# Reordering the rounds of the context-and-routing stage of a fused attention and mixture-of-experts kernel

## The chip, the core and the metric

The kernel runs on one core of a Trainium2 chip. The metric is the device time of one launch in microseconds (us). A core has five engines, each with an instruction queue of its own that it works through in order: TensorE (PE in the profile, its weight loads PEld), VectorE (DVE), ScalarE (ACT), GpSimd (POOL) and SyncE (SP, which here only issues transfers). Engines wait for one another through semaphores.

## What is computed

Tokens x are 32 sequences of 56 rows of 256 numbers; each sequence has a context of 1500 x 256. Four steps follow one another, each added to x:

1. A decayed scan over the context, projected in and out and averaged over time. Since everything in it is linear, it is one weighted sum of the 1500 context rows per sequence, times one 256 x 256 matrix, plus a constant row. The normalized x plus this row is normalized again.
2. A mixture of 16 experts (hidden width 176); every token goes to its best 6 of 16 by a softmax gate.
3. Attention of the tokens over their own context, with a mask.
4. A mixture of two experts (hidden width 1024), one per token.

```
x = x + layernorm(layernorm(x) + mean_t(scan(ctx W_in + b_in) W_out + b_out))
x = x + sum over the best 6 of 16 of score_e * expert_e(layernorm(x))
x = x + softmax(layernorm(x) ctx^T / 16, masked) ctx
x = x + score_best * expert_best(layernorm(x))
```

## The kernel before, in words

The change lies in the first stage, which does step 1 and sorts the tokens for step 2. Its loop runs over 16 pairs of sequences (`for p in range(NP)`, lines 653 to 697); a pair is a tile of 128 rows, 56 tokens in each half. The steps of one pair are spread over several rounds of the loop, and each round calls steps of pairs p, p-1, p-2 and p-3:

- `count_in(b)`, L350: PE sums the 1500 rows of context b with the scan's weights into `acc` in PSUM, 12 matmuls. Contexts lie in a ring of five buffers in SBUF; after context b has been summed, SP issues the load of context b+5 (1536 KB in the profile, L165).
- `sum_out` (ScalarE copies `acc` out, L478), `sum_in_columns` (PE `sp` L484, then `sv`), `projected` (PE `sT` L497, ScalarE `sm` L501), `to_rows` (PE `bp` L505, the row spread to 128 rows).
- `first_stats` and `first_rows`: the first normalization of x, on DVE with two ScalarE roots (Ln, then Exp), and on GpSimd `z` L470 and `xr` L474.
- `first_norm` (DVE `z` L509, statistics L189 and L190, two roots on ScalarE), `residual` (DVE L516, L517, statistics), `second_root` (ScalarE), `second_norm` (GpSimd `xn` L529), `away` (SP stores `xn` to DRAM, L535).
- `turned` (PE transposes `xn`, `tp` L201, ScalarE copies `xT` L203), `gate` (PE `lp` L543), `best` (ScalarE copies the logits L552; DVE takes the six best; ScalarE takes `pr`, an Exp that needs DVE's maximum, L563).
- `ranks` (PE `rk` L568), `counted` (DVE), `places` (DVE, with one scaling on ScalarE): each chosen token's place in its expert's list, as a level and an offset in a block of 128.
- `ones_at(p, h)`: one-hot rows of the offsets, half h of the experts; half 0 and half of half 1 on DVE (L609), the other four experts on GpSimd (L614). `sorted_in` (PE, `owned` L631): one-hots times values, summed over all pairs into the table of blocks.

After the loop come the last pair's steps and the tables of the sorted blocks (lines 698 to 780); then the expert stage gathers rows of `xn` from DRAM (`xb` L956) and multiplies them by the up weights (`gu` L798) and the down weights (`y` L825). The up weights are loaded by four transfers (`load_w0_up`, L214), the down weights by 26 small ones (`w0_down_pieces`, L233).

Within one engine the order of the instructions is what sets the order of the work. PE, DVE, ScalarE and SP run in the order in which the code is written (`manual_schedule`, L90); for GpSimd a scheduler chose the order in the first stage. It put `z` and `xr` of a later pair ahead of `xn` in each round.

Of the kernel before, what the change touches and what calls it, by code (L numbers as in the profile page):

```python
# [19 lines left out]
P = 128  # L20
# [32 lines left out]
LATE = T - WIN  # L53
SPAN = 2048
FAR = 1 << 17
ISC = 1.0 / 16.0


@with_exitstack
def xattn_ffn_kernel(  # L60
# [178 lines left out]
    with tc.tile_pool(name="p1", bufs=1) as p1, tc.tile_pool(name="p3", bufs=3) as p3, tc.tile_pool(  # L239
# [160 lines left out]
                start=(e == 0), stop=False,  # L400
            )
        PE.matmul(vp[:, 0:D], lhsT=ones[0:1, :], rhs=bout_sb, start=False, stop=True)
        cvec = p1.tile([1, D], F32, name="cvec")
        A.copy(cvec, vp[0:1, 0:D])

        sm = p1.tile([3, D], F32, name="sm")
        nc.gpsimd.dma_start(out=sm[2:3], in_=cvec)
        t3 = p1.tile([P, 3], F32, name="t3")
        V.tensor_scalar(t3[:, 0:1], lower, -1.0, 1.0, ALU.mult, ALU.add)
        V.tensor_copy(t3[:, 1:2], lower)  # L410
# [48 lines left out]
        rsa = p1.tile([P, NP], F32, name="rsa")  # L459

        def first_stats(o):
            for p in range(o, o + 4):
                V.bn_stats(out=st[:, p, :], in_=xr[:, p, :])
                V.bn_aggr(out=mva[:, p, :], in_=st[:, p, :])
            inverse_root(rsa[:, o : o + 4], mva[:, o : o + 4, 1])

        def first_rows(o):
            for p in range(o, o + 2):
                zc[p] = zp.tile([P, D], F32, tag="z", name="z")
                G.tensor_scalar(  # L470
                    zc[p], xr[:, p, :], mva[:, p, 0:1], rsa[:, p : p + 1],
                    ALU.subtract, ALU.mult,
                )
                G.tensor_tensor(xr[:, p, :], xr[:, p, :], bet, ALU.add)  # L474

        def sum_out(p):
            acc = p3.tile([P, D], F32, tag="acc", name="acc")
            A.copy(acc, pend[p]["acc"][:, 0:D])  # L478
            keep(p, acc=acc)

        def sum_in_columns(p):
            sp = ps.tile([P, 512], F32, tag="ps", name="sp")
            for k in range(KD):
                PE.matmul(  # L484
                    sp[:, 2 * k : 2 * k + 2], lhsT=pend[p]["acc"][:, k * P : (k + 1) * P],
                    rhs=sel2[:, 0:2], start=True, stop=True,
                )
            sv = p3.tile([P, KD, 2], F32, tag="sv", name="sv")
            V.tensor_scalar(
                sv.rearrange("p k h -> p (k h)"), sp[:, 0 : 2 * KD], 1.0 / T, None, ALU.mult  # L490
            )
            keep(p, sv=sv)

# [14 lines left out]
        def first_norm(p):  # L508
            V.tensor_tensor(zc[p], zc[p], pend[p]["bp"][:, 0:D], ALU.add)  # L509
            mv = stats(zc[p])  # L510
            inverse_root(mv[:, 2:3], mv[:, 1:2])
            keep(p, mv=mv)

        def residual(p):
            mv = pend[p]["mv"]
            V.scalar_tensor_tensor(zc[p], zc[p], mv[:, 0:1], gam, ALU.subtract, ALU.mult)  # L516
            V.scalar_tensor_tensor(  # L517
                xr[:, p, :], zc[p], mv[:, 2:3], xr[:, p, :], ALU.mult, ALU.add
            )
            keep(p, mv=stats(xr[:, p, :]))  # L520
# [45 lines left out]
        def ranks(p):  # L566
            rk = ps.tile([P, 512], F32, tag="ps", name="rk")
            PE.matmul(rk[:, 0:E0], lhsT=before, rhs=sel[:, p, :], start=True, stop=True)  # L568
            PE.matmul(rk[:, E0 : 2 * E0], lhsT=ones, rhs=sel[:, p, :], start=True, stop=True)
            keep(p, rk=rk)  # L570

        def counted(p):

            rk = pend[p]["rk"]
            V.tensor_tensor(pos[:, p, :], rk[:, 0:E0], base0, ALU.add)
            V.tensor_tensor(base0, base0, rk[:, E0 : 2 * E0], ALU.add)

        def places(p):

            nm, pr = pend[p]["nm"], pend[p]["pr"]  # L580
            qi = small.tile([P, E0], I32, tag="qi", name="qi")
            V.tensor_copy(qi, pos[:, p, :])
            V.tensor_scalar(qi, qi, 7, None, ALU.logical_shift_right)
            V.tensor_copy(lvl[:, p, :], qi)

            off = small.tile([P, E0], F32, tag="off", name="off")
            V.scalar_tensor_tensor(
                off, lvl[:, p, :], -float(P), pos[:, p, :], ALU.mult, ALU.add
            )
            V.scalar_tensor_tensor(off, off, 1.0, sel[:, p, :], ALU.add, ALU.mult)  # L590
            v = vals[:, p % 2]
            V.tensor_tensor(
                v[:, :, 0, :], e16.unsqueeze(1).to_broadcast([P, E0, NLP]),
                lvl[:, p, :].unsqueeze(2).to_broadcast([P, E0, NLP]), ALU.is_equal,
            )
            V.reciprocal(nm[:, 1:2], nm[:, 1:2])
            V.scalar_tensor_tensor(
                v[:, :, 1, :], v[:, :, 0, :], nm[:, 1:2],
                pr.unsqueeze(2).to_broadcast([P, E0, NLP]), ALU.mult, ALU.mult,
            )  # L600
            A.activation(v[:, :, 0, :], v[:, :, 0, :], AF.Copy, scale=ids[:, p : p + 1])
            keep(p, off=off)

        def ones_at(p, h):

            off = pend[p]["off"][:, NE * h : NE * h + NE]
            oh = ohp.tile([P, NE, P], F32, tag="oh", name="oh")
            n = NE // 2 if h and p < NP - 1 else NE
            V.tensor_tensor(  # L609
                oh[:, 0:n], iota.unsqueeze(1).to_broadcast([P, n, P]),  # L610
                off[:, 0:n].unsqueeze(2).to_broadcast([P, n, P]), ALU.is_equal,
            )
            for i in range(n, NE):
                G.tensor_scalar(oh[:, i, :], iota, off[:, i : i + 1], None, ALU.is_equal)  # L614
            pend[p].setdefault("hots", []).append(oh)

        def busy(n):

# [19 lines left out]
        lgs = [p1.tile([P, E0 + 2], F32, name=f"lg{i}") for i in range(2)]  # L638
        for lg in lgs:
            G.memset(lg[:, E0 : E0 + 2], -BIG)  # L640
        sum_out(0)
        first_stats(0)
        first_rows(0)
        pieces = list(w0_down_pieces())


# [3 lines left out]
                    pieces.pop(0)()  # L650


        for p in range(NP):
            if p >= 1:
                first_norm(p - 1)
            if p >= 3:
                ones_at(p - 3, 0)
            if p >= 1:
                residual(p - 1)
            if p >= 2:  # L660
                count_in(2 * p)
                count_in(2 * p + 1)
            if p >= 1:
                sum_out(p)
                second_root(p - 1)
            if p >= 2:
                ranks(p - 2)
            sum_in_columns(p)
            if p >= 3:
                ones_at(p - 3, 1)  # L670
            if p >= 1:
                second_norm(p - 1)
                away(p - 1)
                some_pieces(1)
            projected(p)
            if p >= 3:
                sorted_in(p - 3)
            if p >= 1:
                turned(p - 1)
            if p >= 2:  # L680
                counted(p - 2)
                places(p - 2)
            if p >= 1:
                gate(p - 1)
            to_rows(p)
            if p < 3:
                first_stats(4 * p + 4)
            if p == 2:
                table_constants()
            if p >= 1:  # L690
                best(p - 1)
            if p % 2 == 0 and p + 2 < NP:
                first_rows(p + 2)
            if p == NP - 3:
                load_w0_up()
            if p > NP - 3:
                some_pieces(6)
        last = NP - 1
        first_norm(last)
        ones_at(NP - 3, 0)  # L700
        residual(last)
        ones_at(NP - 3, 1)
        second_root(last)
        ranks(NP - 2)
        second_norm(last)
        away(last)
        some_pieces(len(pieces))
        sorted_in(NP - 3, 0)
        turned(last)
        sorted_in(NP - 3, 1)  # L710
        gate(last)
        busy(1)
        counted(NP - 2)
        places(NP - 2)
        best(last)
        ranks(last)
        for h in range(2):
            ones_at(NP - 2, h)
        for h in range(2):
            sorted_in(NP - 2, h)  # L720
        counted(last)


# [7 lines left out]
        at_ = vals[:, NP % 2]  # L731
# [209 lines left out]
    with tc.manual_schedule(  # L941
# [30 lines left out]
        def ways(a, b):  # L972
# [6 lines left out]
            for l in range(levels_of(b - 1)):  # L979
# [8 lines left out]
                ra[:, q], ra[:, q], float(P), pos[:, q], ALU.mult, ALU.add  # L988
            )
            yield lambda: V.scalar_tensor_tensor(  # L990
                ra[:, q], ra[:, q], 1.0 - P, sel[:, q], ALU.add, ALU.mult
            )
            for p in range(a, b):
                yield lambda p=p: V.max(out=t8s[:, p, :], in_=ra[:, p, :])
# [702 lines left out]
```

## Time and profile before

| what | value |
|---|---|
| median of 3 runs | 728.69 us (727.43 to 730.54) |
| the profiled execution: its time | 726.86 us |
| its span, first to last instruction | 725.2 us |
| busy in the span: PE, PEld, DVE, ACT, POOL | 662.7, 441.0, 402.1, 241.8, 348.7 us |
| mean granted PE clock, of full speed | 0.954 |
| count of pair 2 ends, count of pair 15 ends | 52.3 and 175.4 us |
| first gate and up matmul of the expert stage | 209.05 us |
| between these two counts: DMA share, GB/s, PE clock | 0.95, 345, 0.93 |

The profile's page cuts the span into 40 slices of 18.1 us; the first ten are the loop. "DMA" is the mean busy share of the 16 DMA engines, "PEclk" the granted clock of PE, both in tenths in the page. The chain of waits follows the work that ended last back through the engines; the waits list who waited for whom ("43.1, 11, 6.0" is 43.1 us in total, 11 times, 6.0 us the longest).

### The profile page before, as it was taken

To read this page: it belongs to the slowest core of one execution; us is meant where nothing else is said; L and a number is where in the kernel's file an instruction comes from. 1 tells how busy PE (TensorE), PEld (TensorE's weight loads), DVE (VectorE), ACT (ScalarE), POOL (GpSimd) and SP (SyncE) were. 2 spreads that over 40 slices of the span, in tenths; PEclk is the share of its full clock that TensorE was granted. 3 is DMA by queue.
4 is the path that set the end of the run, shared out by engine and by line. 5 is a ranking of instruction groups with operands and counts; after the bars stand their busy time and mean duration, and the time that the engine had idled before them with its cause. 6 is when DMAs were issued, how large, how long until landed. Compare 5 with 4: busy or idle time off the path is not lost.

```text
span 725.2 us, 13538 instructions
## 1 busy us (share of the span) xinstructions
PE 662.7 (91%) x4113; PEld 441.0 (61%) x4113; DVE 402.1 (55%) x1378; ACT 241.8 (33%) x704; POOL 348.7 (48%) x440
## 2 busy tenths in 40 slices
PE   7867888888779999999999999999988999999996
PEld 4534555555447777667777776666644656656664
DVE  7548877788815645535444447677876332322322
ACT  0123333333124444444444443566551111111110
POOL 7164665554154457567766776568342202212111
PEclk8869998999579999999999999999999999999999
DMA  8998999899527999545554554796931201111000
GB/s 313 309 358 344 369 358 339 320 387 306 152 66 232 266 331 294 172 137 158 152 154 131 163 156 132 204 290 128 351 127 52 58 8 44 29 31 43 22 30 18
DMA packets 70657, 136.62 MB, mean 188 GB/s; under 512 B 7732, under 2 KB 43205, under 8 KB 70581
## 3 DMA queue, kind: packets, MB, share of 16 engines
q1 hardware_dynamic: 56036, 100.31, 40.2%
q0 software_dynamic: 14544, 35.37, 18.3%
q8 instruction: 38, 0.62, 0.4%
q14 instruction: 39, 0.31, 0.1%
HBM read 109.54 MB, written 26.77 MB: 188 GB/s over the span
## 4 chain that ended last, share of the span: by engine, by line
PE 79%; DVE 11%; POOL 3%; ACT 3%; issue 2%; DMA 2%; POOLq 0%; DVEq 0%
PE gu L798 29%; PE y L825 18%; PE acc L360 7%; PE tp L816 5%; PE tp L201 4%; PE tp L926 2%; PE sp L1155 2%; PE owned L631 2%; PE op L1190 1%; PE bp L505 1%; PE lp L543 1%; DVE st L189 1%; POOL xn L529 1%; DVE oh L609 1%; DMA sm<-cvec 1%
## 5 line engine op out<-in xcount | busy, mean ns | idle before, releaser
L798 PE MATMUL gu<-w_sb,xT 128*128 x380 | 131.1, 467 | 3.5 <-issue 1.3
L804 ACT ACTIVATE sg<-gu 128x176 f32<-128x176 f32 (+1 forms) x155 | 53.2, 343 | 229.8 <-PE gu L798 225.9
L956 POOL DMA_INDIRECT xb<-xn,idx x95 | 91.4, 962 | 62.4 <-PE tp L201 39.3
L798 PE MATMUL gu<-ring,xT 128*128 x240 | 112.9, 593 | 0.6 <-issue 0.6
L810 DVE SCALAR_TENSOR_TENSOR hs<-sg,wgt,gu 128x176 f32<-128x176 f32 x95 | 37.7, 397 | 120.3 <-ACT sg L804 120.3
L825 PE MATMUL y<-w_sb,hT 88*128 x380 | 97.9, 379 | 0.0
L798 PEld LDWEIGHTS gu<-w_sb,xT 128*128 128x128 f32 x380 | 71.5, 192 | 30.6 <-ACT xT L203 2.9
L869 POOL DMA_INDIRECT g<-ys,early x78 | 74.6, 956 | 30.0 <-issue 14.7
L808 DVE TENSOR_TENSOR hs<-sg,gu 128x256 f32<-128x256 f32 x60 | 25.2, 420 | 112.2 <-ACT sg L804 112.2
L1441 POOL DMA_INDIRECT out<-ob,ti x15 | 14.8, 989 | 127.2 <-DVE ob L1438 126.9
L816 PEld LDWEIGHTS tp<-ident,hs 128*88 128x88 f32 (+1 forms) x310 | 39.9, 130 | 58.7 <-issue 46.7
L825 PEld LDWEIGHTS y<-w_sb,hT 88*128 88x128 f32 x380 | 64.5, 190 | 5.7 <-issue 0.6
L798 PEld LDWEIGHTS gu<-ring,xT 128*128 128x128 f32 x240 | 45.3, 190 | 33.1 <-issue 30.2
L818 DVE COPY hT<-tp 88x256 f32<-88x256 f32 (+1 forms) x155 | 64.3, 415 | 0.2 <-PE tp L816 0.2
L825 PE MATMUL y<-ring,hT 128*128 x240 | 61.7, 380 | 0.0
L203 ACT COPY xT<-tp 128x256 f32<-128x256 f32 x126 | 47.0, 373 | 44.0 <-PE tp L201 43.0
L816 PE MATMUL tp<-ident,hs 128*88 128x128 f32 (+1 forms) x310 | 59.3, 273 | 0.2 <-DVE mv L884 0.2
L360 PE MATMUL acc<-ring,cz 128*32 128x256 f32 x768 | 53.5, 434 | 0.2 <-DVE cz L321 0.2
L964 ACT COPY yb<-y 128x256 f32<-128x256 f32 x95 | 35.4, 372 | 42.8 <-PE y L825 41.4
L201 PE MATMUL tp<-ident,xb 128*128 128x128 f32 x220 | 42.3, 274 | 2.3 <-issue 2.3
L825 PEld LDWEIGHTS y<-ring,hT 128*128 128x128 f32 x240 | 41.0, 190 | 3.3
L360 PEld LDWEIGHTS acc<-ring,cz 128*32 128x32 f32 x768 | 27.4, 124 | 24.0 <-issue 11.6
(309 smaller groups left out, 1007.1 us busy)
## 6 DMA issues: line engine op xcount, KB each, us to landing
ring<-in_cx SPq DMA_DIRECT2D x32, 1536.0 KB
ys<-yb SPq DMA_DIRECT2D x95, 128.0 KB
ring<-in_cx SPq DMA_DIRECT2D x16, 384.0 KB
extra<-in_cx SPq DMA_DIRECT2D x16, 384.0 KB
xs<-zrow SPq DMA_DIRECT2D x5, 771.0 KB
w_sb<-in_wg SPq DMA_DIRECT2D x2, 1408.0 KB
w_sb<-in_wu SPq DMA_DIRECT2D x2, 1408.0 KB
xn<-xn SPq DMA_DIRECT2D x16, 128.0 KB
```

The costliest lines, as they stand in the source:

```text
L201: PE.transpose(tp[:, k * P : (k + 1) * P], xn[:, k * P : (k + 1) * P], ident)
L203: A.copy(xT.rearrange("p k c -> p (k c)"), tp[:, 0 : KD * P])
L360: PE.matmul(acc[Q * g : Q * g + Q, 0:D], lhsT=cz[:, j, 1 - h : 1 - h + Q], rhs=c[:, j, :], start=(h == 0 and m == 0), stop=(h == 1 and m = ...
L798: PE.matmul(gu[:, 0 : 2 * fp], lhsT=xT[i][:, k, :], rhs=w[:, bass.ds(at[i] + (u * piece + k * 2 * fp), 2 * fp)], start=(k == 0), stop=(k = ...
L804: A.activation(sg, gu[:, 0:fp], AF.Silu)
L810: V.scalar_tensor_tensor(hs[i, u], sg, wgt[:, i : i + 1], up, ALU.mult, ALU.mult)
L816: PE.transpose(tp[0:h, c * P : (c + 1) * P], a[:, c * h : (c + 1) * h], ident)
L818: V.tensor_copy(hT[i, u], tp[0:h, 0 : 2 * P])
L825: PE.matmul(y[i][:, 0:D], lhsT=a[:, c * P : (c + 1) * P], rhs=w[0:h, bass.ds(at[i] + (u * piece + doff + c * D), D)], start=(u == 0 and c ...
L869: G.indirect_dma_start(out=g, out_offset=None, in_=ys0[0 : n * P, :], in_offset=bass.IndirectOffsetOnAxis(ap=at[:, p, k : k + 1], axis=0),)
L956: G.indirect_dma_start(out=xb, out_offset=None, in_=xn0, in_offset=bass.IndirectOffsetOnAxis(ap=idx[:, i : i + 1], axis=0),)
L964: A.copy(yb, y[:, 0:D])
```

## The change

Each round's calls are put in another order, and parts of the steps are changed:

- GpSimd's order in the loop is fixed, as written: `xn`, one-hots, then `z` and `xr` of pair p+2.
- The contexts of pair p+1 are summed in round p, in two pieces: the first between `projected` and `to_rows`, the second after `residual`. Before, both contexts of pair p were summed in one piece in round p.
- `to_rows` and `first_norm` of pair p come in the middle of round p, `residual(p)` behind them; before, `first_norm` and `residual` of pair p-1 stood at the start of round p.
- `sum_out(p)` is the first call of a round. The call before it is the end of the round before: `best`, then `first_stats` (now two pairs in each of rounds 0 to 6, not four pairs before the loop and in rounds 0 to 2).
- `sorted_in` is called by halves.
- All pieces of the down weights come in rounds 13 to 15 and behind them; before, one came in each of rounds 1 to 15, six more in each of rounds 14 and 15, and what was left after that. The up weights are issued in round 12, not 13.
- The bias row goes straight into `sm` by one ScalarE copy of three rows, without a transfer.
- Level and offset of a place are worked out by adding and subtracting a large constant in float; the casts to integer and the shift go. Positions are multiplied by `sel` at once and count from one.
- `sv` is made on ScalarE, not on DVE.
- After the loop the steps of pairs 13 to 15 are reordered too; one of the four spare matmul groups (`busy`) goes, and a scratch tile lies in the context ring.

The core of the diff:

```
-        cvec = p1.tile([1, D], F32, name="cvec")
-        A.copy(cvec, vp[0:1, 0:D])
-
         sm = p1.tile([3, D], F32, name="sm")
-        nc.gpsimd.dma_start(out=sm[2:3], in_=cvec)
+        A.copy(sm, vp[0:3, 0:D])
...
         def first_stats(o):
-            for p in range(o, o + 4):
+            for p in range(o, o + 2):
...
-            V.tensor_scalar(
-                sv.rearrange("p k h -> p (k h)"), sp[:, 0 : 2 * KD], 1.0 / T, None, ALU.mult
+            A.activation(
+                sv.rearrange("p k h -> p (k h)"), sp[:, 0 : 2 * KD], AF.Copy, scale=1.0 / T
             )
...
-            V.tensor_tensor(pos[:, p, :], rk[:, 0:E0], base0, ALU.add)
+            V.scalar_tensor_tensor(
+                pos[:, p, :], rk[:, 0:E0], 1.0, base0, ALU.add, ALU.add
+            )
+            V.tensor_tensor(pos[:, p, :], pos[:, p, :], sel[:, p, :], ALU.mult)
...
-            qi = small.tile([P, E0], I32, tag="qi", name="qi")
-            V.tensor_copy(qi, pos[:, p, :])
-            V.tensor_scalar(qi, qi, 7, None, ALU.logical_shift_right)
-            V.tensor_copy(lvl[:, p, :], qi)
-
+            V.tensor_scalar(lvl[:, p, :], pos[:, p, :], -0.5 - P / 2, ROUND, ALU.add, ALU.add)
+            V.tensor_scalar(lvl[:, p, :], lvl[:, p, :], -ROUND, 1.0 / P, ALU.add, ALU.mult)
...
-            V.scalar_tensor_tensor(off, off, 1.0, sel[:, p, :], ALU.add, ALU.mult)
...
+        p1x.enter_context(
+            tc.manual_schedule(engines={ET.PE, ET.DVE, ET.Activation, ET.SP, ET.Pool})
+        )
+        first_stats(0)
+        for p in range(2):
+            first_rows(p)
         for p in range(NP):
+            sum_out(p)
             if p >= 1:
                 second_root(p - 1)
+                second_norm(p - 1)
+                away(p - 1)
             sum_in_columns(p)
             if p >= 3:
                 ones_at(p - 3, 1)
+                sorted_in(p - 3, 0)
+            if p >= 2:
+                ranks(p - 2)
             projected(p)
+            if 2 <= p + 1 < NP:
+                count_in(2 * p + 2)
             if p >= 2:
                 counted(p - 2)
                 places(p - 2)
+            to_rows(p)
+            if p >= 1:
+                turned(p - 1)
+            first_norm(p)
+            if p >= 3:
+                sorted_in(p - 3, 1)
+            if 2 <= p < last:
+                ones_at(p - 2, 0)
             if p >= 1:
                 gate(p - 1)
+            if p == last:
+                ones_at(p - 2, 1)
+            residual(p)
+            if 2 <= p + 1 < NP:
+                count_in(2 * p + 3)
             if p >= 1:
                 best(p - 1)
+            if 2 * p + 2 < NP:
+                first_stats(2 * p + 2)
+            if p + 2 < NP:
+                first_rows(p + 2)
+            if p == 7:
+                table_constants()
+            if p == NP - 4:
                 load_w0_up()
+            if p > NP - 4:
                 some_pieces(6)
```

(The lines of the loop without a plus stand in both versions, at other places in the one before.)

More of the change, by code (lines that the diff above doesn't have):

```diff
@@ L55 @@
 FAR = 1 << 17
+ROUND = 1.5 * float(P << 23)
 ISC = 1.0 / 16.0
@@ L461, in first_stats, with first_rows @@
         def first_stats(o):
-            for p in range(o, o + 4):
+            for p in range(o, o + 2):
                 V.bn_stats(out=st[:, p, :], in_=xr[:, p, :])
                 V.bn_aggr(out=mva[:, p, :], in_=st[:, p, :])
[L465 to L474, printed above, removed]
+            inverse_root(rsa[:, o : o + 2], mva[:, o : o + 2, 1])
+        def first_rows(p):
+            zc[p] = zp.tile([P, D], F32, tag="z", name="z")
+            G.tensor_scalar(
+                zc[p], xr[:, p, :], mva[:, p, 0:1], rsa[:, p : p + 1], ALU.subtract, ALU.mult
+            )
+            G.tensor_tensor(xr[:, p, :], xr[:, p, :], bet, ALU.add)
         def sum_out(p):
@@ L614, in ones_at @@
                 G.tensor_scalar(oh[:, i, :], iota, off[:, i : i + 1], None, ALU.is_equal)
-            pend[p].setdefault("hots", []).append(oh)
+            pend[p].setdefault("hots", {})[h] = oh
         def busy(n):
@@ L640, in xattn_ffn_kernel @@
             G.memset(lg[:, E0 : E0 + 2], -BIG)
-        sum_out(0)
-        first_stats(0)
-        first_rows(0)
         pieces = list(w0_down_pieces())
@@ L650, in some_pieces @@
                     pieces.pop(0)()
+        last = NP - 1
+        p1x.enter_context(
+            tc.manual_schedule(engines={ET.PE, ET.DVE, ET.Activation, ET.SP, ET.Pool})
+        )
+        first_stats(0)
+        for p in range(2):
+            first_rows(p)
         for p in range(NP):
+            sum_out(p)
             if p >= 1:
[L655 to L664, printed above, removed]
                 second_root(p - 1)
-            if p >= 2:
-                ranks(p - 2)
+                second_norm(p - 1)
+                away(p - 1)
             sum_in_columns(p)
@@ L670, in xattn_ffn_kernel @@
                 ones_at(p - 3, 1)
[L671 to L674, printed above, removed]
+                sorted_in(p - 3, 0)
+            if p >= 2:
+                ranks(p - 2)
             projected(p)
[L676 to L679, printed above, removed]
+            if 2 <= p + 1 < NP:
+                count_in(2 * p + 2)
             if p >= 2:
@@ L682, in xattn_ffn_kernel @@
                 places(p - 2)
+            to_rows(p)
[6 more added lines that the diff above has]
+                ones_at(p - 2, 0)
             if p >= 1:
                 gate(p - 1)
[L685 to L689, printed above, removed]
+            if p == last:
[3 more added lines that the diff above has]
+                count_in(2 * p + 3)
             if p >= 1:
                 best(p - 1)
-            if p % 2 == 0 and p + 2 < NP:
+            if 2 * p + 2 < NP:
+                first_stats(2 * p + 2)
+            if p + 2 < NP:
                 first_rows(p + 2)
-            if p == NP - 3:
+            if p == 7:
+                table_constants()
+            if p == NP - 4:
                 load_w0_up()
-            if p > NP - 3:
+            if p > NP - 4:
                 some_pieces(6)
[L698 to L702, printed above, removed]
         second_root(last)
-        ranks(NP - 2)
+        ranks(last - 1)
         second_norm(last)
@@ L707, in xattn_ffn_kernel @@
         some_pieces(len(pieces))
-        sorted_in(NP - 3, 0)
+        sorted_in(last - 2, 1)
         turned(last)
-        sorted_in(NP - 3, 1)
+        counted(last - 1)
         gate(last)
-        busy(1)
-        counted(NP - 2)
-        places(NP - 2)
+        ones_at(last - 2, 0)
         best(last)
+        sorted_in(last - 2, 0)
         ranks(last)
+        places(last - 1)
         for h in range(2):
-            ones_at(NP - 2, h)
+            ones_at(last - 1, h)
         for h in range(2):
-            sorted_in(NP - 2, h)
+            sorted_in(last - 1, h)
         counted(last)
@@ L730, in xattn_ffn_kernel @@
         )
-        at_ = vals[:, NP % 2]
+        at_ = slots[B % NRING].rearrange("p j d -> p (j d)")[0:1, CW - 2 * E0 * NLP :]
+        at_ = at_.rearrange("p (e o l) -> p e o l", e=E0, o=2)
         V.scalar_tensor_tensor(
@@ L990, in ways @@
             yield lambda: V.scalar_tensor_tensor(
-                ra[:, q], ra[:, q], 1.0 - P, sel[:, q], ALU.add, ALU.mult
+                ra[:, q], ra[:, q], -float(P), sel[:, q], ALU.add, ALU.mult
             )
```

## The prediction

> **What bounds the kernel now.** I read the 40 slices first, then the waits of the first stage, the chain of waits over one of its rounds, and that round in order of time. All edits lie in the first stage, which ends where the first gate and up matmul starts, at 209.05 us in the chain; behind it stand 516 us of expert and attention work that the edits don't touch and that can only shift. The page:
>
> ```profile
> PEclk8869998999579999999999999999999999999999
> DMA  8998999899527999545554554796931201111000
> GB/s 313 309 358 344 369 358 339 320 387 306 152 66 232 266 331 294 172 137 158 152 154 131 163 156 132 204 290 128 351 127 52 58 8 44 29 31 43 22 30 18
> ```
>
> The DMA engines look full for ten slices (181 us). They are not the bound. Five-microsecond stretches show what they can do and that they fall below it:
>
> ```profile
> 95.00:100.00 5.00, 4.54 (x75) 2.95 (x70) 3.84 (x17) 2.25 (x8) 3.01 (x5) 1.00 1.02 419
> 115.00:120.00 5.00, 4.90 (x38) 2.46 (x42) 3.74 (x12) 1.53 (x7) 1.47 (x3) 0.58 0.80 311
> ```
>
> The last three columns are granted clock, DMA share and GB/s. A round of two contexts moves 2 x 1.573 MB, plus 0.13 MB written: 7.9 us at 415 GB/s. The rounds take 9.2 us. And PE does not wait for the contexts (40 to 200 us):
>
> ```profile
> POOL z L470 <- DVE xr L517: 43.1, 11, 6.0
> ...
> ACT acc L478 <- PE acc L360: 16.8, 13, 3.6
> ...
> PEld acc L360 <- DMA ring<-in_cx: 0.3, 1, 0.3
> ```
>
> 0.3 us in all for the context ring. The round is a circle through the in-order engines:
>
> ```profile
> 107.15 2.77 PE acc L360 x48
> ...
> 110.83 0.44 DVE st L189
> 111.36 0.18 DVE mv L190
> ...
> 111.59 0.61 DVE oh L609
> ...
> 112.21 0.73 POOL xr L474
> 112.94 1.22 POOL xn L529
> ...
> 114.20 0.46 PE tp L201 x2
> ...
> 115.10 0.62 PE lp L543 x4
> 115.72 1.00 PE bp L505 x2
> 116.72 5.28 PE acc L360 x48
> ```
>
> GpSimd's xn is held up by the z and xr of a later pair that the scheduler put ahead of it; PE queues bp and the two counts behind tp and lp, which need xn. DVE is nearly full too: from one z (98.41) to the next (107.61) it idles 1.12 us, waiting for the gate's logits.
>
> **The change, edit by edit.** The profiled execution took 726.86 us with a span of 725.2; the sum is made on that span. The median of the runs, 728.69, lies 1.8 above it.
>
> *Bias row.* The copy through DRAM of cvec goes (6.21 us in the chain). Only bp(0) waited for it, 2.29 us; contexts were arriving at 335 to 410 GB/s meanwhile. See "start" below.
>
> *DVE's arithmetic.* The three cast and shift operations of `places` (0.57, 0.20 and 0.26 us; with gaps 1.14 from 112.39 to off at 113.53), the off product (0.20) and sv (0.05) go; two scalings and one product of 0.17 each and gaps (0.6) come. DVE's own work per round falls from 9.2 - 1.12 = 8.1 us to 7.3. Where `first_stats` runs (now two pairs in each of rounds 0 to 6, before, four pairs ahead of the loop and in each of rounds 0 to 2) it is 1.1 more, 8.4. No gain by itself: a round is set by its longest circle.
>
> *Order of the round.* Here the time is decided. In the new order each engine's queue is fixed, GpSimd's too, and ScalarE's ends a round with: logits, `pr` (an Exp that needs DVE's maximum), then the two roots of `first_stats` in rounds 0 to 6, and only then the copy of the next pair's sums out of PSUM. DVE makes that maximum after `residual`, so nearly at its end of the round. PE's next work (sp) waits for the copy, the row bp waits behind sp, rk, sT and one count, and DVE's z waits for bp. One circle, no part beside another:
> - DVE from z to the end of `residual`, the 1024-wide one-hot within it: 107.61 to 111.46 = 3.85
> - maximum to start of pr: 106.77 to 107.23 = 0.46; pr with its accumulator read 0.40
> - copy to sp 109.94 to 110.37 = 0.43; sp 0.56
> - sorted half: 32 records of `owned` take 1.93 at clock 0.50, so 16 at full clock 0.48; rk 0.50
> - sT, four passes of 0.215 = 0.86 (sv on ScalarE, not in the trace, 128x4: between 0.13, as on DVE, and 0.36, as the sm copy; I take 0.2; hidden behind the sorted half and rk either way)
> - one count, half of the 2.73 = 1.37; bp to z 0.75 (0.69 and a hop)
>
> Sum 9.66 us. With the statistics: maximum to end of sel 0.84, four statistics 1.17, a hop 0.10, two roots 0.56, instead of 0.86: 1.81 more, 11.5; I take 11.4. The same way of adding puts the old circle at 9.24 where the rows show 9.20, so I trust these to 0.2. The wait of GpSimd (43.1 us) does go: the new order has 5.5 us of GpSimd work per round (1.22 + 2.36 + 1.23 + 0.73) with slack. What is late next is ScalarE's copy.
>
> Old: pair 2's count ended at 52.3, pair 15's at 175.4, 13 rounds, 123.1 us. New: six with statistics (the first without the one-hot, -1.1) 67.3, and seven of 9.66 = 67.6; 134.9. That is +11.8.
>
> *Start.* z(0) comes 2 us sooner, but pair 1's copy then stands behind residual(0) and statistics of pairs 2 and 3 in ScalarE's queue; sp(1) starts near 41.9 instead of 40.1, and PE is at half clock there as before. Count of pair 2 ends near 53: +0.7.
>
> *Clock.* With full speed in all rounds the old 13 would have taken 11 x 9.2 + 2 x 8.5 = 118.2; drops cost 4.9 already. [...] between the second count and sp it idles 2.5 us in rounds without statistics and 4.3 with (its work from sp on is 0.56 + 0.48 + 0.50 + 0.86 + 1.37, bp 0.55, tp 0.40, the other sorted half 0.48, lp 0.55 and 1.37: 7.1 us)[...]. The rows speak for more: the clock fell to 0.50 at 117.5 to 122.5 (and near 65, 88 and 137) though PE had not idled over 0.7 us; what came before was a quiet stretch of some 3 us (tp, lp, bp). The new quiet stretch, idle plus sp, is 3.1 or 4.9 us. I follow the rows: about seven drops of 4 us at half clock, 2 us each on the circle, 14; less what the old 4.9 suggests is hidden (1.2 per drop), I take 9, with 0 and 35 as ends.
>
> *Down weights.* 26 pieces of 0.84 us issue now all stand behind the up weights in SP's queue, xn stores among them. Pair 13's store waits with them, 18 pieces (15 us) stand ahead of pair 15's store and 8 (7 us) behind. From the end of round 12: up weights 13.2 us of issue (163.05 to 176.21), a store of up to 3.8, then 26 pieces and stores: done near 40 us. The first gather comes near 49 us after that point, the first down matmul 8 later. Cost 0; 15 early pieces leave the context stream (1.1 MB), worth nothing where contexts aren't waited for. If rounds were fast this cover would be gone first (8 us of slack left at 8 us a round).
>
> *Tail.* From the last residual to the first gate matmul it was 23.6 us (185.5 to 209.05). `places(14)` moves behind best(15) onto the path (+1.0); shorter `places(15)` gives 0.3 back, round 15 without counts 0.3: +0.4. One warm-up matmul less: the clock was 0.50 there with it.
>
> Sum: 0.7 + 11.8 + 9 + 0.4 = +21.9; 725.2 + 21.9 + 1.7 = 748.8. I say 749.
>
> **Rivals.**
> 1. *The transfers become the bound, faster.* If ScalarE's copy did not wait for the end of DVE's round, a round would be set by DVE's 8.4 or 7.3 us or the transfer's 7.9: from 53, six of 8.4 and seven of 7.9 end at 158.7, 16.7 us sooner, 710. For it: GpSimd's 43 us wait goes and PE counts ahead. Against it: the queue order. It decides if the circle comes under 9.47 us on average (123.1 / 13), 0.9 below my mean of 10.38.
> 2. *The clock stays low, far slower.* At clock 0.55 the PE part (4.5 us) of the circle takes 8.2: with that in every round with statistics and every third other, 6 x 3.5 + 2.5 x 3.7 = 30 in place of 9: 770.
> 3. *It comes out even.* The statistics' roots hurt less than counted, the late rounds run at the old 9.2, and no drops: within 4 us of 728.7.
>
> **Numbers.** Forecast 0.74, rival 1 0.07, rival 2 0.10, rival 3 0.09. Range: without more drops and 0.2 less a round, 725.2 + 10.3 + 1.7 = 737; up to 766 it holds the forecast and the near half of rival 2. About 0.5% (3.6 us) is what a measurement can tell from no change: faster 0.06, same 0.08, slower 0.86.
>
> **What would show it.** In the profile after: pair 15's count ending near 195 instead of 175; rounds near 11.4 up to pair 8 and near 9.7 from there; ScalarE's sum copy right behind pr or the statistics' roots, with PE's sp waiting for ScalarE some 2 to 4 us a round; GpSimd's wait for xr gone; PEclk lower in slices 3 to 6; DMA share below the old in those slices. The expert stage the same length. Wrong if sp starts directly after the second count, if the context ring shows up as PE's wait, or if the first gather waits for pair 15's store.

## The result, and the profile after

The changed kernel takes 778.85 us (median of 4 runs, 776.19 to 780.9), the kernel before 728.06 us beside it: a ratio of 1.069, 95% interval 1.065 to 1.074. It is slower, as forecast, but by 51 us instead of 20, and outside the range. The profiled execution took 776.19 us with a span of 774.5. The profiled executions of experiments 8, 10 and 11 below were disturbed early in the loop, so only the durations of their tails are used.

Where the 49.3 us of span come from, by the same marks as in the sum of the prediction:

| stretch | before | after | difference | forecast |
|---|---|---|---|---|
| start to the end of pair 2's count | 52.3 | 53.5 | +1.2 | +0.7 |
| from there to the end of pair 15's count, 13 rounds | 123.1 | 166.3 | +43.2 | +20.8 (rounds 11.8, clock 9) |
| from there to the first gate and up matmul | 33.65 | 38.9 | +5.3 | +0.4 |
| the rest | 516.1 | 515.7 | -0.4 | 0 |

The slices of the profile after, of which the first twelve (19.4 us each) are now the loop:

```profile
PEclk7857567787865999999999999999999999999999
DMA  8996665766962388974555456488881200110100
```

Before, the granted clock dipped in places (6 tenths in one of the ten slices, 8 or 9 in the others); now all of these twelve slices stand at 8 tenths or below, and the DMA share falls from 8 and 9 tenths to mostly 6. Three rounds of the profile after (stretch, length, busy time of PE, PEld, DVE, ACT and POOL, then granted clock, DMA share, GB/s): one with the statistics, the worst one, and one without statistics.

```profile
71.20:85.10 13.90, 9.98 (x101) 5.84 (x100) 8.24 (x29) 3.53 (x14) 5.53 (x8) 0.75 0.61 238
85.10:100.30 15.20, 13.84 (x101) 7.25 (x100) 8.29 (x29) 3.65 (x14) 5.56 (x8) 0.50 0.57 189
176.80:188.70 11.90, 9.86 (x101) 5.64 (x100) 6.91 (x24) 2.99 (x12) 6.21 (x10) 0.79 0.81 305
```

Every one of the twelve rounds looked at in this way stands between 0.73 and 0.79, but for the one at 0.50; summed over the twelve (twice the missing share times the length) that is 81 us at half clock. The five rounds with statistics from 57 to 129 us take 14.4 us on average, the seven behind them 11.95.

Who waited for whom between 52 and 225 us, after (in total, times, longest):

```profile
POOL xn L525 <- ACT mv L197: 106.5, 14, 9.8
PEld sp L480 <- ACT acc L474: 41.5, 14, 4.4
...
PE sp L480 <- ACT acc L474: 34.0, 14, 4.0
ACT pr L559 <- DVE m L554: 32.6, 14, 2.6
```

GpSimd no longer waits for `xr`; it waits for the root ahead of `xn`, idle because the round is long, and no one waits for the context ring. The new wait is the one forecast: PE's `sp` for ScalarE's copy of the sums (acc L474), every round, and ScalarE's `pr`, ahead of that copy, for DVE's maximum. One round of the chain of waits, after (start, us, what):

```profile
184.56 0.40 ACT pr L559 x2
184.96 0.27 ACT acc L474
...
185.27 0.77 PE sp L480 x4
186.04 1.01 PE owned L626 x16
187.05 0.54 PE rk L564 x2
187.59 0.43 PE rk L565 x2
188.02 1.37 PE sT L493 x3
...
189.41 0.40 PE sT L493
189.81 2.56 PE acc L361 x21
192.37 0.67 PE bp L501 x2
...
193.06 0.43 DVE z L505
...
197.28 0.40 ACT pr L559 x2
197.68 0.27 ACT acc L474
...
197.99 0.61 PE sp L480 x4
```

This is the circle of the prediction, link by link, with nothing beside it. From `z` (193.06) to the next `sp` (197.99) it takes 4.93 us; the forecast was 5.14. From `sp` (185.27) to `z` it takes 7.79, where the forecast was 4.52. In the next round that part takes 6.26 (197.99 to 204.25); the two lengths alternate, 7.0 on average. So the whole miss of a late round lies in PE's part, where each matmul group takes up to twice what it was given: the sorted half 1.01 instead of 0.48, `rk` 0.97 instead of 0.50, `sT` and the count 4.3 instead of 2.2. The same stretch, cut where the clock changes in this trace (clock, DMA share and GB/s at the end); every change of the clock there lies 3.41 us, or a multiple of it, behind the one before:

```profile
182.16:185.57 3.41, 1.37 (x23) 0.69 (x15) 3.12 (x12) 0.97 (x5) 0.00 (x0) 1.00 1.03 418
185.57:188.99 3.42, 3.42 (x29) 2.31 (x32) 0.93 (x6) 0.25 (x2) 3.23 (x5) 0.50 1.02 419
188.99:192.40 3.41, 3.41 (x27) 1.19 (x19) 1.27 (x5) 0.87 (x2) 2.47 (x3) 0.50 0.16 51
192.40:195.81 3.41, 3.41 (x48) 2.00 (x48) 2.57 (x6) 0.93 (x4) 0.00 (x0) 1.00 0.68 181
195.81:199.22 3.41, 1.38 (x25) 1.02 (x22) 2.35 (x10) 1.23 (x6) 0.75 (x1) 1.00 1.04 392
199.22:202.64 3.42, 3.42 (x26) 1.82 (x30) 1.93 (x9) 0.77 (x2) 3.42 (x6) 0.50 1.19 301
```

PE stands still for 2.04 us ahead of `sp` (195.95 to 197.99, while DVE works), so it is busy for only 1.4 us of the stretch of 3.41 us that holds this wait. At the end of that stretch, about 1.2 us after PE has taken up work again (0.3 us in the round before), the clock falls to half, and `sT` and the count, which `bp` and so DVE wait for, run at it. It stays there for one stretch in one round and for two in the other, which is why the two lengths alternate. And while PE crawls through the count, the context transfers have next to nothing to do (DMA share 0.16 from 188.99 to 192.40): SP issues the next one only when a count has freed a buffer, and waited for that 88.5 us, 22 times, between 52 and 220 us.

### The profile page after: what moved, and what is told of

It is laid out like the page before. It is cut to its first block, busy times and chain, and to the rows that moved or that the text cites. A ratio compares the mean times of both kernels' runs of the same rounds, so it can differ in the third digit from the quotient of the medians.

```text
span 774.5 us, 13504 instructions
## 1 busy us (share of the span) xinstructions
PE 698.5 (90%) x4111; PEld 455.1 (59%) x4111; DVE 398.4 (51%) x1346; ACT 243.4 (31%) x728; POOL 349.2 (45%) x439
## 4 chain that ended last, share of the span: by engine, by line
PE 77%; DVE 15%; ACT 3%; issue 2%; POOL 1%; DMA 0%; DVEq 0%; POOLq 0%; ACTq 0%
PE gu L793 27%; PE y L820 17%; PE acc L361 5%; PE tp L811 4%; PE sT L493 4%; PE tp L202 3%; DVE oh L604 2%; DVE st L190 2%; PE tp L921 2%; PE owned L626 2%; PE sp L1150 2%; PE sp L480 2%; PE op L1185 2%; PE bp L501 2%; DVE xr L513 1%
## 5 line engine op out<-in xcount | busy, mean ns | idle before, releaser
L793 PE MATMUL gu<-w_sb,xT 128*128 x380 | 128.9, 461 | 3.6 <-ACT xT L204 2.2
L361 PE MATMUL acc<-ring,cz 128*32 128x256 f32 x768 | 77.0, 505 | 0.2 <-DVE cz L322 0.2
L525 POOL TENSOR_SCALAR xn<-xr,mv 128x256 f32<-128x256 f32 x15 | 18.3, 1220 | 106.5 <-ACT mv L197 106.5
L361 PEld LDWEIGHTS acc<-ring,cz 128*32 128x32 f32 x768 | 32.6, 133 | 27.1 <-issue 19.3
L480 PE MATMUL sp<-sel,acc 128*128 128x2 f32 x64 | 13.2, 310 | 39.1 <-ACT acc L474 39.0
```

Source lines behind the costliest of these rows:

```text
L361: PE.matmul(acc[Q * g : Q * g + Q, 0:D], lhsT=cz[:, j, 1 - h : 1 - h + Q], rhs=c[:, j, :], start=(h == 0 and m == 0), stop=(h == 1 and m = ...
L793: PE.matmul(gu[:, 0 : 2 * fp], lhsT=xT[i][:, k, :], rhs=w[:, bass.ds(at[i] + (u * piece + k * 2 * fp), 2 * fp)], start=(k == 0), stop=(k = ...
```

## The experiments

The first four kernels ran on a chip on which the kernel before took 778.21 us (773.88 to 782.72); what is longer there is the stage behind the first gate matmul (556 to 570 us in the four profiled runs, instead of 516). They are compared by their ratio to the kernel before on that chip, and by the first gate matmul's start in their own profile (before 209.05, after 258.76). That the first stage takes as long on both chips is taken from two things: 778 less 556 to 570 leaves 206 to 220 for the kernel before, and the late rounds of experiment 3 there (11.2 and 12.7 us in turn, from `sp` to `sp`) are as long as those of the changed kernel, within 0.03 us. All others ran where the kernel before took 727 to 729 us.

**1. The copy alone, earlier.** The next pair's `sum_out` goes from the head of its round to right behind the second count, so ahead of `best` and the statistics in ScalarE's queue:

```
         for p in range(NP):
-            sum_out(p)
...
                 count_in(2 * p + 3)
+            if p + 1 < NP:
+                sum_out(p + 1)
             if p >= 1:
                 best(p - 1)
```

> The changed kernel with one call moved: the copy of the next pair's sums out of PSUM stands directly behind the second count, ahead of the gate's logits, the Exp and the statistics' roots in ScalarE's queue. Theory A (the round's length comes from ScalarE's queue: PE's next work waits for ScalarE, which waits for the end of DVE's round; the clock only adds to it): sp then follows the count directly, and the circle closes through sv, which still stands behind the Exp and the roots: 3.85 + 0.46 + 0.40 + 0.52 + 0.2 + 0.86 + 1.37 + 0.75 = 8.4 us, 10.2 with statistics, against 9.66 and 11.4; the 13 measured rounds shrink by 1.2 us each at full clock and about 1.8 at the clock of the changed kernel: 755 to 765 us. Theory B ([...] the clock stays low whatever ScalarE does): rounds stay at 12 and 14 us, 775 to 780.

Measured: 1.0115 of before (1.0061 to 1.0169); first gate matmul at 218.3, 40.5 us sooner than after, where theory A expected 14 to 24. This one call's place is four fifths of the loss. It gives back more than the wait is worth, since the clock comes back too: from 97 to 174 us the page (slices of 19.4 us) shows 9 tenths or more.

```profile
PEclk7879599998599999999999999999999999999999
```

**2. The wait kept, the clock bought.** Three spare 128x512 matmuls (two in rounds 7 to 15), which nobody reads, behind the second count, in PE's idle time ahead of `sp` (two of them took 1.99 us there, three 2.85 in most rounds):

```
                 count_in(2 * p + 3)
+            spare(3 if p < 7 else 2)
```

> The changed kernel with spare matmuls of 128x512, whose results nobody reads, behind the second count of each round (three in rounds 0 to 6, two in the others; 0.9 us each at full clock), in the time in which PE waits for ScalarE. Theory A with the clock as its second part: the granted clock stays near full and the rounds fall to the lengths of the forecast, 9.7 and 11.4 us: 13 rounds take 135 us instead of 166, the tail keeps its 39: 745 to 750 us. If the clock is not what makes the rounds 2.3 us longer than the sum of their parts, nothing falls, 775 to 785, or it rises where the spare matmuls themselves delay PE.

Measured: 1.0242 of before (1.0178 to 1.0305); first gate matmul at 231.3, 27.5 us sooner than after. ScalarE's copy still comes last, the order is the changed kernel's to the letter. The late rounds take 10.07 us instead of 11.95, the clock is 1.00 in them and 0.86 to 0.94 in those with statistics. A late round of this kernel's chain:

```profile
169.81 0.61 PE sp L480 x4
170.42 0.57 PE owned L634 x16
171.00 0.32 PE rk L564 x2
171.32 0.22 PE rk L565 x2
171.54 0.74 PE sT L493 x3
...
172.50 1.29 PE acc L361 x21
173.79 0.64 PE bp L501 x2
...
174.46 0.43 DVE z L505
```

PE's part is 4.65 us (174.46 - 169.81), against 4.52 in the forecast and 7.0 in the changed kernel: the working of the circle was right, for a clock that the change doesn't leave it. So at least 27.5 of the 49.7 us are the price of the clock in this order: 22.0 in the 13 rounds (144.3 us instead of 166.3) and 5.1 behind them (33.8 us instead of 38.9, with the same code there). That the time, 746 us by the ratio, lies in the expected range is in part luck: the rounds took more than the expected 135 us, the tail less than the expected 39.

**3. The statistics off ScalarE's path.** `first_stats` goes from behind `best` to behind `projected`:

```
             projected(p)
+            if 2 * p + 2 < NP:
+                first_stats(2 * p + 2)
...
                 best(p - 1)
-            if 2 * p + 2 < NP:
-                first_stats(2 * p + 2)
```

> The changed kernel with the statistics of the next two pairs moved from the end of the round (behind best, ahead of the copy of the sums) to the middle (behind the row's projection), where DVE waits for the ranks. Theory A: rounds 0 to 6 lose the 1.8 us that statistics and roots put on the circle, and become as long as the later ones, 11.9 instead of 14.2: six times 2.3, 14 us less, 763 to 767 us. Theory B or a circle that does not run through ScalarE's roots: no change, 776 to 780.

Measured: 1.0413 (1.0332 to 1.0495); first gate matmul at 245.1, 13.7 us sooner. Rounds with statistics take 9.6 to 14.0 us (from `z` to `z`), 12.3 on average, near the others; the late rounds stay at 11.95 and the clock low (0.899 of full speed over the profiled execution, 0.902 in the changed kernel). The statistics' roots ahead of the copy cost what was counted, about 2 us in each of six rounds, and are not the main loss. (The gains of experiments 1 to 4 overlap and can't be added.)

**4. Copy and columns early, statistics in mid-round.**

```
+        sum_out(0)
+        sum_in_columns(0)
         for p in range(NP):
-            sum_out(p)
...
-            sum_in_columns(p)
+            projected(p)
             if p >= 3:
                 ones_at(p - 3, 1)
                 sorted_in(p - 3, 0)
+            if 2 * p + 2 < NP:
+                first_stats(2 * p + 2)
...
                 count_in(2 * p + 3)
+            if p + 1 < NP:
+                sum_out(p + 1)
+                sum_in_columns(p + 1)
             if p >= 1:
                 best(p - 1)
-            if 2 * p + 2 < NP:
-                first_stats(2 * p + 2)
```

> The changed kernel with the circle cut: copy of the sums, sp and sv of the next pair directly behind the second count, sT the first thing of the round, the statistics in the middle of the round. Theory A: PE's part no longer waits for the end of DVE's round but for the ranks: 3.85 + 0.94 + 0.5 + 1.37 + 0.75 = 7.4 us, or DVE's own 7.3 (8.4 with statistics), or the transfers' 7.9, whichever is longest: six rounds of 8.6 and seven of 8.0 after 53 us put pair 15's count at 161 instead of 220, PE hardly idles, the clock holds, and the time is 710 to 725 us, below the kernel before. Theory B: PE works 7.1 us per round at half to three quarters of its clock, 10 to 12 us a round: 750 to 775 us.

Measured: 0.9923 of before (0.9892 to 0.9955); first gate matmul at 201.3, 57.5 us sooner than after and 7.8 sooner than before. Two stretches of its rounds:

```profile
60.00:69.00 9.00, 8.06 (x105) 4.78 (x100) 8.33 (x28) 3.37 (x15) 5.92 (x8) 1.00 1.02 406
...
118.00:136.00 18.00, 16.14 (x204) 9.55 (x200) 13.88 (x49) 5.83 (x24) 13.85 (x15) 1.00 0.97 368
```

The rounds take about 9.0 us, with and without statistics, at clock 1.00, although the counts still come in two pieces: so the two pieces are not by themselves what keeps it low. PE's longest wait in a round is now 0.5 us. The DMA share is 1.0, but the transfers are not what bounds a round: PE doesn't wait for the ring, while SP waits for PE's counts (40.3 us, 18 times, from 53 to 170 us). The chain shows what does, a circle through GpSimd:

```profile
149.16 1.23 POOL xn L525
150.39 2.57 POOL oh L609 x4
153.00 0.41 PE owned L626 x2
153.41 0.55 PE lp L539 x4
153.95 1.48 PE acc L361 x24
155.45 0.38 ACT acc L474
```

GpSimd's one-hots stand behind its `xn`, and PE's queue holds the sorted matmuls that need them ahead of the logits and the second count. So the rounds stop at 9.0, not at the 8.0 to 8.6 expected here or the 7.9 of rival 1 of the prediction; the time, 722 us by the ratio, is still within the expected 710 to 725.

**5. GpSimd's order alone, in the kernel before.** The order of all engines is fixed as written, `xn` right behind the second root, `z` and `xr` one pair per round:

```
-        def first_rows(o):
-            for p in range(o, o + 2):
+        def first_rows(o, n=1):
+            for p in range(o, o + n):
...
+        p1x.enter_context(
+            tc.manual_schedule(engines={ET.PE, ET.DVE, ET.Activation, ET.SP, ET.Pool})
+        )
...
                 second_root(p - 1)
+                second_norm(p - 1)
```

> The kernel before with one part of the change alone: GpSimd's order in the loop fixed, xn first, then the one-hots, then z and xr of one pair per round. Theory A: the wait of GpSimd for xr is not what sets a round; with it gone the old circle shortens by the 0.3 to 0.7 us by which the late rounds without z were shorter (8.5 against 9.2): 11 rounds, 3 to 8 us less than the kernel before, 0.989 to 0.996 of it. If the fixed order were the cost of the change, it would be slower than the kernel before.

Measured: 1.0419 of before (1.0371 to 1.0467), a miss in sign. First gate matmul at 240.8; rounds of 11.3 to 12.3 us (from `z` to `z`). The wait for `xr` is gone, and its place is taken by another:

```profile
DVE m L554 <- ACT lg L552: 36.1, 11, 4.7
PEld owned L631 <- POOL oh L614: 21.6, 38, 1.3
```

A round's sorted matmuls now wait for one-hots that GpSimd makes behind the `xn` of the same round, and PE's queue holds these matmuls ahead of `xn`'s transposes and the logits: `tp` starts 2.7 us after the end of `xn` (115.59, 112.85), where in the kernel before it starts 0.06 us after it (105.01, 104.95). There the one-hots had been made a round ahead, and no sorted matmul waits for GpSimd. So the fixed order costs more by its one-hots than it gains by its `xn`. What `xn` ahead of `z` and `xr` would be worth with the one-hots left a round ahead was not tried: `xr` and `xn` stand in the old chain (0.73 and 1.22 us a round), so it is not shown that GpSimd's 43.1 us were mere slack.

**6. The small edits, in the kernel before**: bias row without a transfer, places without casts, `sv` on ScalarE (as in the diff of the change).

> The kernel before with the small edits alone, in the old order: the bias row without a transfer, level and offset without casts, sv on ScalarE. Theory A: no part of the loss. The start gains up to 2 us, each round up to 0.4 us on DVE beside a wait of 1.1 us: 0 to 7 us less, 0.990 to 1.000 of the kernel before. If one of them (sv behind the roots in ScalarE's queue) were at fault, above 1.005.

Measured: 1.0122 of before (1.0087 to 1.0157), a miss in sign for theory A; the fault that it named (above 1.005) is there. PE, late in the loop, has a gap that the kernel before doesn't have:

```profile
126.29 0.61 PE L482 MATMUL sp<-sel,acc 128*128 128x2 f32 x4
128.15 1.44 PE L495 MATMUL sT<-wc,sv 128*2 128x256 f32 x3 [1.25 <-ACT sv L487]
```

In the old order ScalarE has the second root ahead of `sv`, and waits for its statistics; 15.7 us of PE's weight loads for `sT` wait on it in the loop.

**7. The up and down weights as before** (the pieces one per round, the up weights in round 13), in the changed kernel:

```
+                 some_pieces(1)
...
-            if p == NP - 4:
+            if p == NP - 3:
...
-            if p > NP - 4:
+            if p > NP - 3:
```

> The changed kernel with the down weights' pieces as before: one in each of rounds 1 to 15, the up weights in round 13, the rest behind. Forecast and theory A: no cost and no gain, since nothing waits for these transfers in the changed kernel; its first stage stays 259 us within 2. If the late pieces hold up the last stores of xn, or if their absence feeds the contexts sooner, it differs by 3 us or more.

Measured: 1.0644 of before (1.0603 to 1.0685), 775.8 us; first gate matmul at 260.7 (the changed kernel: 1.069 with overlapping intervals, 258.76). The place of the pieces is worth nothing within what can be told.

**8. The tail, first try**, in the kernel of experiment 4: pair 14's `best` and `ranks` ahead of the last residual, its `counted` and `places` behind it.

```
+                best(p - 1)
+                ranks(p - 1)
             residual(p)
...
+            if p == last:
+                counted(p - 1)
+                places(p - 1)
...
-        ranks(last - 1)
...
-        counted(last - 1)
...
-        places(last - 1)
```

> The version with the circle cut (copy, sp and sv early, statistics in mid-round), and pair 14's best, ranks, counts and places brought back ahead of or beside the last residual. Theory A for the tail: places(14), 1.9 us, and the ranks on PE, 1.0 us at half clock, leave the path behind the last gate: 2 to 3 us less than the version with the circle cut, whose first stage took 201.3 us: 198 to 199.5, 0.985 to 0.990 of the kernel before where that one had 0.992. If the tail is set by PE's half clock alone, within 1 us of it.

Measured: 0.9904 of before (0.9875 to 0.9934), the same as without it; in the profile the tail (from pair 15's count to the first gate matmul) is 39.0 us, 2.1 longer than in experiment 4. ScalarE took the scaling of `places(14)` ahead of the last pair's second root, and the root waited (from 181.8, when its statistics were there, to 184.1 us). A miss.

**9. The small edits without `sv`** (experiment 6 with `sv` left on DVE).

```
-            A.activation(
-                sv.rearrange("p k h -> p (k h)"), sp[:, 0 : 2 * KD], AF.Copy, scale=1.0 / T
+            V.tensor_scalar(
+                sv.rearrange("p k h -> p (k h)"), sp[:, 0 : 2 * KD], 1.0 / T, None, ALU.mult
             )
```

> The kernel before with two of the change's small edits (the bias row without a transfer, places without casts), and sv left on VectorE, unlike the run of the small edits. Theory: the small edits' loss of 1.2% came from sv standing behind the second root in ScalarE's queue, where TensorE waited for it (17.0 us of waits of sT on sv): without it the time is 0.990 to 1.002 of before, and the rounds of the first stage are again near 9.3 us with no wait of sT on ScalarE. Rival: it came from the other two edits or from the order that the planner makes with the new durations: then it stays near 1.012.

Measured: 0.998 of before (0.9953 to 1.0007), 726.06 us. So the loss of experiment 6 was `sv`, an instruction of 0.13 us on DVE moved to a queue where it stands behind a root. In the changed kernel it stands behind the copy, and PE doesn't wait for it: there "hidden either way" was right. The other two edits are worth nothing to the time.

**10 and 11. The tail, second try, and its control on the same chip.** Experiment 11 is experiment 4 unchanged; experiment 10 has one call elsewhere behind the loop:

```
         counted(last - 1)
+        places(last - 1)
         gate(last)
...
         ranks(last)
-        places(last - 1)
```

> The run of copy and columns early, once more, unchanged, beside the kernel before on this call's chip. Theory: its gain comes from the first stage alone (7.8 us shorter than before's), which does not depend on the chip: about 6 to 8 us less than before, 0.989 to 0.992; first gate matmul near 201 us from the span's start, clock 1.00 in every round. Rival: the gain was that chip's: 0.997 or more.

> The changed kernel with the copy and columns of the next pair directly behind the second count (the run of copy and columns early), and in the tail the places of the last pair but one directly behind its count, ahead of the last pair's ranks. Theory: the places' 1.9 us leave the path between the last ranks and the last selection, and the last selection starts some 2 us earlier: 1 to 3 us less than the same kernel without it in the same call, so 0.983 to 0.991 of before. Rival: the last pair's ranks are late by as much as the places take, so the end doesn't move: same within 1 us.

Measured: experiment 11 0.9919 of before (0.9879 to 0.9959), so the gain of experiment 4 holds on a second chip; experiment 10 0.9861 (0.9835 to 0.9886), 717.64 us, the fastest kernel here, and faster than both. In the profiles the tail is 31.8 us in experiment 10 and 35.3 in 11. The tail is shorter as expected, by 3.5 instead of some 2 us; by the times alone the two are not told apart with certainty, since the intervals overlap.

**12. Is a round locked to the spacing of the clock's changes?** In the changed kernel two late rounds take 23.9 us, which is seven times 3.41 us, the shortest spacing of the clock's changes in its profile (the "window" of the expectation). Two more small statistics on DVE (0.27 us each, read by nobody) in rounds 7 to 15 make the circle longer by about 0.55 us:

```
+            if p >= 7:
+                pause()
             if p >= 1:
                 best(p - 1)
```

> The changed kernel with two further VectorE statistics of 128x128 (each some 0.25 us, half as wide as those of 0.43 us in the trace; nobody reads their result) between the residual and the logits' maximum in rounds 7 to 15, so with a circle longer by about 0.5 us in the late rounds. Theory A, the round is locked to the clock's window (two rounds of 23.87 us are seven windows of 3.41 us): the late rounds stay at 11.95 us on average, and the time moves by less than 1 us. Theory B, the length of a round is the sum of its parts and the ratio of seven is chance: the late rounds become 12.4 to 12.5 us, and the first gate matmul comes 3 to 4 us later than in the changed kernel (258.8 to near 262).

Measured: six late rounds of 12.4 to 12.8 us and one of 14.3, the first gate matmul at 265.4, 1.0776 of before (1.0721 to 1.0832). The six grow by 0.65 us on average, near the 0.55 that was put in, so no number of such spacings holds the length of a round: that two rounds made seven is chance, and that idea falls. The round of 14.3 us is one at half clock throughout:

```profile
153.75:166.45 12.70, 10.28 (x106) 5.56 (x101) 7.54 (x29) 3.02 (x12) 5.29 (x7) 0.77 0.68 250
166.45:180.75 14.30, 13.81 (x106) 7.27 (x101) 7.29 (x27) 3.25 (x12) 6.50 (x10) 0.50 0.57 201
```

It is the twin of the 15.2 us round of the changed kernel.

## Why the prediction was wrong in size

**Start.** +1.2 us against +0.7: right.

**Order of the round.** Right, and the reason for the sign: with the clock largely bought back the kernel is still slower than before (experiment 2, 1.0242). The copy of the sums behind `pr`, `sp` behind the copy, `bp` behind one count: all there in the chain, with PE's waits at `sp` of 2.04 us in late rounds and about 3.9 in most with statistics, as written ("some 2 to 4 us a round"). At full clock a late circle is 4.65 (experiment 2) plus 4.93 (the changed kernel) = 9.58 us; 9.66 was forecast. The statistics' share, 1.8 us a round, fits experiment 3 (2.3 a round, at the low clock). And experiment 1 shows that the place of the copy, with the clock that it costs, is 40.5 of 49.7 us.

**Clock.** This step failed. It read: "about seven drops of 4 us at half clock, 2 us each on the circle, 14; less what the old 4.9 suggests is hidden (1.2 per drop), I take 9". The runs show a drop in every round, 81 us at half clock in twelve rounds where the step counted 28. What it cost: in the late rounds 7 x (11.95 - 9.58) = 16.6 us; in the six with statistics 82.6 measured against 67.3 forecast, 15.3 more, if 11.4 is right for their full-clock length. (Experiment 2 has 12.5 there at a mean clock of about 0.9, so the full-clock length lies between the two.) Together up to 32 us instead of 9, and at least the 22.0 that experiment 2 bought back in these rounds with matmuls whose results nobody reads. Two things were wrong in the step:
- It counted drops by how often the kernel before had them. But there the quiet stretch was one event among rounds that differ; the new order puts the same wait, with the same few small matmuls behind it, into every round, so what happens in one happens in all. The prediction had the rows that say so (a drop without an idle of over 0.7 us; a new quiet stretch of 3.1 us) and halved them. (That reading holds for the drops at 88, 117 and 137 us; ahead of the one near 65 PE had idled 1.20 and 1.49 us, more like the new wait.)
- It took part of each drop for hidden. The 1.2 us are what a drop had cost before (4.9 over four), in a circle in which PE was not the link everywhere. In the new one PE's stretch from `sp` to `z` is on the circle whole, and in the late rounds little is hidden: 36 us at half clock are 18 us of PE's time lost, and 16.6 of them show.

In the late rounds PE was idle for 2.04 us ahead of `sp`, where the prediction had 2.5, and the clock fell to 0.50 behind each of these waits. Rival 2 ("the clock stays low", 770 us, chance 0.10) named this case and priced it at 30 us; with the tail's true cost it would have come to 775. It deserved the larger chance, and the range should have held it whole.

**Tail.** +5.3 us against +0.4. Its parts: the last residual comes 0.8 later behind the count (10.9 us, before 10.1); from there to the last selection 6.2 us instead of 4.9, since `ranks` and half a `sorted_in` stand ahead of `turned` in PE's queue, at half clock (0.50 from 230 to 250 us); `places(14)` on DVE's path 1.3 (forecast 1.0); and the matmuls `bl` 3.73 us instead of 2.02. The sum is 5.1. The chain after, and that of experiment 11, which has the same code behind the loop:

```profile
249.23 3.73 PE bl L758 x16
252.96 0.21 PE ep L771
253.17 2.12 PE d L616 x4
```

```profile
201.62 2.02 PE bl L761 x16
203.76 1.72 PE d L616 x4
```

Experiment 11 shows that the missing spare group is not enough to explain 3.73: without it too, `bl` can take 2.02 us; experiment 4, the same kernel, has 3.73. Which of the two happens was not tried further. But the forecast's order behind the loop was right here too: experiment 2, with the changed kernel's code there and two spare matmuls in round 15, takes 33.8 us for this stretch, near the 34.05 of the forecast. So most of the tail's miss goes with the low clock again (0.50 in the changed kernel from 230 to 250 us), which the prediction priced for the rounds alone.

**Down weights, GpSimd, `sv`.** The pieces cost nothing, as forecast (experiment 7); pair 15's store went out at 232.4 us and the gather came at 254.1. GpSimd's wait went. The reading that the old circle had been held up by it is not borne out: with GpSimd's order fixed and the rest as before, the kernel gets slower (experiment 5); but the one-hots moved with it, so the question stays open. And the prediction counted GpSimd's one-hots as work with slack; they are the link at which the circle of experiment 4 stops.

## What to carry to other kernels

When a new order puts the same PE wait into every pass of a loop (here 2.04 us of 11.95, at a granted clock of 0.78 to 0.79), price the low clock in every pass, on all the matmuls that lie on the circle, and give the case in which the clock stays low the main chance, not a corner. Follow the short instruction that a long queue hides: here a 0.3 us copy behind another engine's last step cost 40 us, and a 0.13 us scaling behind a root cost 10 to 12. An engine that waits 43 us is not by that alone a link to take out; try its new order in the old kernel, one move at a time, before counting on it.

## What had not been expected of the hardware

In the changed kernel the granted clock fell to 0.50 in every round with PE idle for 2.04 us at a stretch out of 11.95, and stayed there for 3.4 or 6.8 us although PE was busy throughout; with that idle time cut to 0.6 us by two spare matmuls (experiment 2), or to 0.5 us by the order (experiment 4), the late rounds ran at 1.00. PE's busy time ahead of a fall doesn't settle it alone: in the kernel before PE was busy for 2.29 us of the 3.41 from 74.87 to 78.28 us, and as long from 85.11 to 88.52, and the clock stayed at 1.00 behind the first stretch and stood at 0.50 behind the second (to 91.93). What decides is not shown here. One chip took 40 to 54 us longer for the stage behind the first gate matmul, which none of these edits touch: in experiment 1 there, PE's gate and up matmuls of the first experts waited 33.0 us in all, in the changed kernel 3.6. Why was not looked into.
